# A graph layer on one core: 16 neighbour slots per batch looked up by TensorE in place, features as three 16-bit terms, kept edges on ScalarE

## The chip, the cores and the metric

The kernel runs on 1 core of one Trainium2 chip. The core has five engines with a queue each, which run their instructions in order and wait for each other through semaphores: TensorE (PE in the profile; its weight loads, PEld, overlap its matmuls), VectorE (DVE), ScalarE (ACT), GpSimd (POOL), and SyncE (SP), which issues most transfers. Matmuls write to eight banks of PSUM; everything else lies in SBUF or in the device's memory. The metric is the device time of one execution in microseconds (us). The kernel before takes 1395.76 us, the median of 3 runs (1393.39 to 1398.31).

## The reference

There are 16 graphs of 1024 nodes with 64 features each; the matrix `adj` holds about 8 neighbours per node. Shortened:

```python
h = relu(layernorm(x))                       # per node, 64 features
neigh = (adj > 0) & ~eye
nb = neigh.sum(-1); rank = cumsum(neigh) - neigh
skip = where(nb > 10, (nb + 1) // 2, 1)
rem = neigh & (skip > 1) & (rank % skip == skip - 1) & mask[:, :, None]
rem = rem | rem.T                            # edges dropped, both ways
nd = (neigh | eye) & ~rem                    # what is kept, the node itself included
s = sort(where(nd, h[neighbour], inf))       # per node and feature, over its kept neighbours
agg = 0.25 * quantile(s, .25) + 0.5 * quantile(s, .5) + 0.25 * quantile(s, .75)
y = relu((h + agg) @ W1 + b1) @ W2 + b2
return x + y * mask
```

So for every node the features of its kept neighbours are fetched, sorted for each of 64 features, and combined with weights that depend on the number of neighbours.

## The kernel before

The work goes batch by batch (a batch is one graph, 0 to 15), and two batches make a pair, 0 to 7. A batch is *prepared* and a pair gets its *results*; the results of one pair run beside the preparation of the next but one.

**Preparation** of a batch (`prepare`). `load` brings in `adj`, takes its signs on ScalarE (L1087) and transposes them by a transfer into `ne`. `drop` ranks the edges on TensorE (`rk`, L1174 and L1179), turns them into a distance on ScalarE (`dist`, L1189) and marks the dropped ones on VectorE (`rem`, L1190). `keep` subtracts the marks from the edges on TensorE (`kp`, L1202 to L1206): half of the results are compared on VectorE against the edges themselves (L1209, where the matmul with `plus` is left out), the other half go through ScalarE (L1213, after that matmul), and both give `kept`, which TensorE packs into codes of 17 numbers per 128 columns (`code`, L1216, copied by L1221). `order` sorts the nodes by their number of neighbours and builds the permutation `perm` (L1259). `normalize` computes the features `xt` and packs them beside the codes into `pack`, as one 16-bit half and two bytes, each as a 16-bit number (192 columns, L1425 and L1426). `collect` multiplies `perm` with `pack` (`codeP`, L1286, 332 columns, one tile of 128 nodes after the other), so that codes, node numbers and features arrive in sorted order, and VectorE's maxima (L1295, L1326) turn the codes into lists of neighbours (`idx`). ScalarE copies the node's own features out (L1299, L1303, L1304).

Sorted in this way, a row tile (0 to 7) holds 128 nodes of like degree. `FULL` is the number of neighbour slots of each row tile, 11 down to 4; row tile 0 has its own buffer `g0`, 1 to 3 share `g1`, 4 and 5 `g4`, 6 and 7 `g6`. Each slot of each row tile of each batch is filled by one **gather**, an indirect transfer that GpSimd issues (L1491, 128 rows of 64 numbers from the table `gtab` in memory), or by TensorE: `choose` does so for 8 slots of row tile 0. It spreads the list entries over the partitions (`rowsT`, L1526; `rows`, L1532), compares them with the node numbers into one-hot matrices (`hot`, L1536, in the buffer `wide`, which `rem` and `perm` use too), and multiplies these with the features (`got`, L1548: for each slot 8 matmuls of 192 columns). ScalarE puts half and bytes together in `stage` (L1565, L1566), and two transfers per batch carry that to `g0`. In the last pair `pick` does the same for 40 slots (L1601 to L1632).

**Results** of a pair (`results`, `aggregate`). VectorE sorts the slots with a network of minima and maxima (L1656 to L1664), ScalarE multiplies the slots in the window of quantiles with their coefficients (L1679), TensorE adds them (`acc`, L1685). The sum, as three 16-bit terms `o`, goes back to the original order (`high`: for each row tile one matmul for two terms on 128 columns of the array, L1813, and one for the third on 64, L1814) and through the two layers (`hp`, L1843; `yp`, L1860). The 32 nodes of highest degree have slots of their own (`gg`, L1906).

**What sets the order.** The program is written with generators that are woven together; then `arrange` takes all instructions, derives which waits for which, assigns costs and places them on the five queues by list scheduling. The order of each queue is then fixed. A gather also waits for its predecessor's issue and, by the `leash`, for an instruction of VectorE or ScalarE that the plan puts 25 us earlier. `opened` puts a tiny write (`pause`, L938) behind most of VectorE's operations. `FILL` names places on TensorE's queue, counted by position, where matmuls are put whose results nobody reads (all of line 914). `over` records whether a row tile has a node with more neighbours than slots or fewer than `LEAST`; if so, a second, slower kernel runs after this one (`dense_layer`).

## Time and profile before

| | |
|---|---|
| median of the runs | 1395.76 us (1393.39 to 1398.31) |
| span of the profiled execution | 1391.1 us, 31056 instructions |
| between its span and the runs' median | 4.7 us |
| mean granted TensorE clock | 0.978 |
| gathers on GpSimd (L1491) | 856, 1066 ns each |
| one-hot comparisons on VectorE (L1536, L1611) | 112 and 40, 489 and 487 ns each |

The profiled execution has no time of its own in the records beside its span; the runs that were timed are others. How to read the rows: a group has its line, engine, operation, what it writes and reads, the shape, the count, the busy time in us and the mean in ns, then the idle time of the engine before it and who ended it. A wait has who waited for whom, the total in us, the number of times and the longest. A window has its length, then for each engine the busy us and in brackets the instructions, then the granted clock, the DMA share and GB/s; a window of one line leaves out the engines that don't run it. A matmul's duration includes the drain of the array, so matmuls that follow each other overlap, and the distance of their starts tells more than their length.

### The profile page before, as it was taken

The numbers are of one execution on the slowest core, as the hardware profiler recorded it, in microseconds if no ns is written. First come the engines' busy times: TensorE is split into PE (matmuls) and PEld (weight loads), VectorE is DVE, ScalarE is ACT, GpSimd is POOL, SyncE is SP. The second block draws the span as 40 slices with busy tenths as digits, with TensorE's granted clock in tenths as the row PEclk, the third lists the DMA queues.
The fourth block names the chain that finished last, engine by engine and source line by source line (L and its number), as shares of the span: only waits on it lengthen the run. The fifth ranks groups of instructions, "written<-read, shape, count | busy, mean of one in ns | idle before, by whom it ended". The sixth has DMA issues, their size and how long they took to land. (4 is left out here: it accounts for less than half of the span.)

```text
span 1391.1 us, 31056 instructions
## 1 busy us (share of the span) xinstructions
PE 1266.4 (91%) x9400; PEld 760.6 (55%) x9479; DVE 1171.7 (84%) x4995; ACT 982.6 (71%) x3158; POOL 954.3 (69%) x895
## 2 busy tenths in 40 slices
PE   6868889899999998999998999889998999999996
PEld 4445566566455645565464646546456656544533
DVE  6849987997899789987897986998999779997963
ACT  6787989899579957997398846779479832552062
POOL 0177775677777776777777766777777767776730
PEclk9999999999999999999999999999999999999997
DMA  7998486585995499569947379762952576165101
GB/s 235 243 257 213 114 217 159 151 210 129 205 188 152 93 208 252 112 147 229 224 91 195 97 146 229 161 175 55 230 105 78 110 167 124 29 109 106 37 15 25
DMA packets 376082, 209.42 MB, mean 151 GB/s; under 512 B 328126, under 2 KB 328674, under 8 KB 375906
## 3 DMA queue, kind: packets, MB, share of 16 engines
q1 hardware_dynamic: 347426, 178.15, 53.7%
q0 software_dynamic: 28480, 29.20, 11.0%
q8 instruction: 76, 1.25, 0.4%
q14 instruction: 100, 0.82, 0.2%
HBM read 105.63 MB, written 42.61 MB: 107 GB/s over the span
## 5 line engine op out<-in xcount | busy, mean ns | idle before, releaser
L1491 POOL DMA_INDIRECT g<-gtab,idx x856 | 912.6, 1066 | 368.0 <-DMA g<-gtab,idx 138.6
L1659 DVE TENSOR_TENSOR g<-g 128x256 f32<-128x256 f32 (+5 forms) x479 | 292.0, 620 | 4.9 <-ACT g L1632 2.0
L1664 DVE TENSOR_TENSOR g<-g 128x384 f32<-128x384 f32 (+5 forms) x479 | 290.8, 619 | 5.3 <-PE acc L1739 4.5
L1679 ACT ACTIVATE g<-g,coef 128x64 f32<-128x64 f32 x896 | 244.9, 354 | 34.4 <-DVE g L1659 19.3
L1087 ACT ACTIVATE signs<-at,near 128x1024 fp8e4<-128x1024 f32 x120 | 138.6, 1163 | 51.6 <-DMA at<-in_adj_dram 43.9
L1286 PE MATMUL codeP<-pack,perm 128*128 128x332 bf16 x1024 | 169.4, 310 | 2.2 <-DVE perm L1259 1.1
L1189 ACT ACTIVATE dist<-rk,bias 128x512 f16<-128x512 f32 x256 | 156.7, 726 | 10.0 <-DVE hot L1536 6.2
L1685 PE MATMUL acc<-g,kf 128*128 128x128 f32 (+4 forms) x528 | 133.5, 376 | 17.7 <-ACT g L1679 15.0
L1286 PEld LDWEIGHTS <-perm 128*128 128x128 bf16 x1024 | 92.4, 99 | 83.6 <-issue 24.7
L1179 PEld LDWEIGHTS <-ne 128*128 128x128 fp8e4 x1024 | 79.9, 98 | 67.8 <-issue 29.7
L1209 DVE SCALAR_TENSOR_TENSOR kept<-kp,ne 128x512 fp8e4<-128x512 f32 x132 | 89.8, 686 | 27.5 <-PE kp L1206 19.4
L1174 PE MATMUL rk<-parts,cnt 128*128 128x512 bf16 x239 | 91.7, 384 | 21.0 <-ACT dist L1189 16.2
L1685 PEld LDWEIGHTS acc<-g,kf 128*128 128x128 f32 x528 | 81.9, 195 | 45.4 <-ACT g L1679 35.5
L1814 PE MATMUL high<-at_p,o 128*64 128x512 bf16 x256 | 102.5, 406 | 4.1 <-issue 4.0
L1206 PE MATMUL kp<-kw,rem 128*128 128x128 fp8e5 x1024 | 104.3, 219 | 0.0
L1179 PE MATMUL rk<-kw,ne 128*128 128x128 fp8e5 x992 | 101.4, 221 | 1.1 <-issue 0.2
L1548 PE MATMUL got<-pack,hot 128*128 128x192 bf16 x896 | 92.8, 256 | 7.8 <-DVE hot L1536 5.3
L1203 PE MATMUL kp<-rem,kw 128*128 128x512 bf16 x256 | 97.2, 380 | 1.6 <-DVE rem L1190 1.0
L938 DVE MEMSET pause<- 128x1 bf16 x1630 | 96.2, 59 | 0.0
L1206 PEld LDWEIGHTS <-rem 128*128 128x128 bf16 x1024 | 75.3, 97 | 37.3 <-issue 1.6
L1190 DVE TENSOR_SCALAR rem<-dist,half 128x1024 bf16<-128x1024 f16 x128 | 64.7, 512 | 34.1 <-ACT dist L1189 28.7
L1813 PE MATMUL high<-at_p,o 128*128 128x512 bf16 x237 | 92.0, 390 | 0.9 <-ACT own L1304 0.5
(236 smaller groups left out, 2426.9 us busy)
## 6 DMA issues: line engine op xcount, KB each, us to landing
at<-in_adj_dram SPq DMA_DIRECT2D x122, 512.0 KB
perms<-perm SPq DMA_DIRECT2D x16, 2048.0 KB
g<-gtab,idx POOLq DMA_INDIRECT x856
xt<-in_x_dram SPq DMA_DIRECT2D x16, 256.0 KB
y<-in_x_dram SPq DMA_DIRECT2D x16, 256.0 KB
gtab<-xt SPq DMA_DIRECT2D x16, 256.0 KB
out_dram<-y SPq DMA_DIRECT2D x14, 256.0 KB
spare<-in_adj_dram SPq DMA_DIRECT2D x6, 512.0 KB
```

The costliest lines, as they stand in the source:

```text
L1087: nc.scalar.activation(signs.bitcast(FP8).rearrange("p (n e) -> p e n", e=2), whole.rearrange("p (e n) -> p e n", e=2), AF.Sign, bias=near ...
L1179: run.append(nc.tensor.matmul(rk[:, s * P:(s + 1) * P], ne[:, s, ts, n], twice[:, :P] if not b and n else upper, start=False, stop=(s == 3 ...
L1189: nc.scalar.activation(to, rk, AF.Abs, bias=bias[:, t:t + 1])
L1203: run.append(nc.tensor.matmul(kp, minus, rem[:, 4 * n:4 * n + 4, ts], start=side, stop=False))
L1206: run.append(nc.tensor.matmul(kp[:, s], rem[:, t, at:at + P], minus, start=False, stop=(s == 3)))
L1286: run.append(nc.tensor.matmul(flat, perm[:, t, k * P:(k + 1) * P], pack[:, t], start=False, stop=(t == NT - 1), skip_group_check=True,))
L1491: ins = nc.gpsimd.indirect_dma_start(out=gathered[m, tiles][:, slot, k - lo, h], out_offset=None, in_=tables[2 * m + h][0], in_offset=bass ...
L1659: nc.vector.tensor_tensor(at(f + k * df, df, many), pa, pb, OP.min if what == "<" else OP.max)
L1664: nc.vector.tensor_tensor(pa if back else pb, pa, pb, OP.max if what == "<" else OP.min)
L1679: nc.scalar.activation(v[:, i, j], v[:, i, j], AF.Copy, scale=w[:, i, j:j + 1])
L1685: nc.tensor.matmul(acc, ident32, lines[:, s], start=False, stop=(s == now[-1] and not ends), skip_group_check=True)
L1814: run.append(nc.tensor.matmul(high[C * (k % 2):C * (k % 2) + C], o[:, k, 2 * C:], one, start=False, stop=(k == NT - 1), skip_group_check=True,
```

## The change

- **Slots.** `SERVED` replaces `EARLY` and `EXTRA`: TensorE looks up 8 slots of row tile 1 and 8 of row tile 2 in every batch but the last two, where it was 8 of row tile 0. The function `served` does it in groups of 8 slots, for `choose` and `pick` alike. The looked-up features go straight into `g1` (`to_lines`); `stage` and its transfers are gone. `g1` keeps two buffers, `g0` goes from two to one. Per pair, 94 gathers are issued in place of 110; in all, 744 in place of 856.
- **Terms.** `split` writes the features as three 16-bit terms whose sum is the feature: a cast on ScalarE, a subtraction on VectorE, twice. The matmuls for the three terms add up in the same 64 columns of the bank. For a lookup that is 24 matmuls of 64 columns for a slot where 8 of 192 stood; for `codeP` 8 of 204 columns and 16 of 64 per row tile where 8 of 332 stood. Two row tiles of `codeP` now share a bank, and one copy takes own features and node numbers out of both.
- **Kept edges.** From batch 1 on all of `kept` goes through ScalarE, with the matmul of `plus` each time; on VectorE remain 12 of 132.
- **One-hot rows.** `hot` has two buffers of its own with four of the eight node tiles each; `dist` and `rows` share three buffers in place of two.
- **Beside these:** `LEAST` rises to the smallest counts, and `places` gives the slots whose coefficient can be other than zero: 800 products in place of 896. The sums of `high` go in fours: four matmuls on the whole array, then four on half of it. `aggregate` takes row tiles 0 to 3 first in every pair. `h1` is computed in place. `FILL` is empty.

On TensorE, where the sums go back to the original order, this stood before:

```order
L1813 LDWEIGHTS o
L1813 MATMUL high<-at_p,o 128x512
L1814 LDWEIGHTS o
L1814 MATMUL high<-at_p,o 64x512
L1813 LDWEIGHTS o
L1813 MATMUL high<-at_p,o 128x512
L1814 LDWEIGHTS o
L1814 MATMUL high<-at_p,o 64x512
L1241 LDWEIGHTS kb
L1241 MATMUL ps<-more,kb 128x192
```

and this stands now (the same matmuls, L1744 in place of L1813 and L1749 in place of L1814):

```order
L1744 LDWEIGHTS o
L1744 MATMUL high<-at_p,o 128x512
L1744 LDWEIGHTS o
L1744 MATMUL high<-at_p,o 128x512
L1744 LDWEIGHTS o
L1744 MATMUL high<-at_p,o 128x512
L1749 LDWEIGHTS o
L1749 MATMUL high<-at_p,o 64x512
L1749 LDWEIGHTS o
L1749 MATMUL high<-at_p,o 64x512
L1749 LDWEIGHTS o
```

The half-array matmuls no longer alternate with the full ones; four of a kind stand together.

In `keep`, VectorE had its comparisons between operations of the sort before:

```order
L1209 SCALAR_TENSOR_TENSOR kept<-kp,ne 128x512
L1664 TENSOR_TENSOR g_9867<-g_9867 128x512
L938 MEMSET pause 128x1
L1209 SCALAR_TENSOR_TENSOR kept<-kp,ne 128x512
L1656 TENSOR_TENSOR g_9867<-g_9867 128x256
L938 MEMSET pause 128x1
L1659 TENSOR_TENSOR g_9867<-g_9867 128x2x256
L938 MEMSET pause 128x1
L1209 SCALAR_TENSOR_TENSOR kept<-kp,ne 128x512
L1664 TENSOR_TENSOR g_9867<-g_9867 128x2x256
```

Now they are ScalarE's, between coefficient products (L1604), the packing of codes (L1184) and the casts of `split` (L1374, L1376):

```order
L1604 ACTIVATE g_11224<-g_11224,coef 128x64
L1374 CAST pack<-xt 128x8x64
L1176 ACTIVATE kept<-kp 128x512
L1184 CAST pack<-code 128x136
L1176 ACTIVATE kept<-kp 128x512
L1376 CAST pack<-xt 128x8x64
L1176 ACTIVATE kept<-kp 128x512 x2
L1184 CAST pack<-code 128x136
L1604 ACTIVATE g_11224<-g_11224,coef 128x64
L1176 ACTIVATE kept<-kp 128x512
L1604 ACTIVATE g_11224<-g_11224,coef 128x64
L1176 ACTIVATE kept<-kp 128x512
```

The comparisons moved to another engine, and that engine's queue now holds all 16 of a batch.

On VectorE the two subtractions of `split` stand among operations of the sort:

```order
L1375 TENSOR_TENSOR xt<-xt,pack 128x512
L1588 TENSOR_TENSOR g_9020<-g_9020 128x384
L906 MEMSET pause 128x1
L1583 TENSOR_TENSOR g_6966<-g_6966 128x2x384
L906 MEMSET pause 128x1
L1583 TENSOR_TENSOR g_9020<-g_9020 128x3x128
L906 MEMSET pause 128x1
L1377 TENSOR_TENSOR pack<-xt,pack 128x8x64
L1588 TENSOR_TENSOR g_6966<-g_6966 128x2x384
```

Three operations of the sort stand between the one and the other.

The diff, cut to its core:

```diff
@@ -65,10 +65,9 @@
 CAPS = (13, 11, 11, 10, 9, 8, 7, 6)
 CLASSES = (((0,), 13), ((1, 2, 3), 11), ((4, 5), 9), ((6, 7), 7))
 
-LEAST = (8, 4, 4, 4, 4, 4, 0, 0)
-EARLY, AHEAD = 8, 20
+LEAST = (10, 9, 8, 7, 4, 4, 4, 0)
+SERVED, AHEAD = (0, 8, 8, 0, 0, 0, 0, 0), 20
 FINAL = (8,4,4,4,0,0,0,0)
-EXTRA = {}
 MANY = 10
 TURN = 1
 
@@ -79,38 +78,7 @@
-FILL = {
...
+FILL = {}
...
                 kp = bank([P, 4, P], F32, name="kp", tag="mx" if b or n else "agg", bufs=3 if b or n else 2)
-                side = bool(b in range(16) and n or not b and t % 2)
+                side = bool(not b and (n or t % 2))
                 run = [] if side else [nc.tensor.matmul(kp, plus, ne[:, :, ts, n], start=True, stop=False)]
                 run.append(nc.tensor.matmul(kp, minus, rem[:, 4 * n:4 * n + 4, ts], start=side, stop=False))
                 for s in range(4):
...
-            owns[b // 2] = wk.tile([P, NT, 2, C], F32, name="own", bufs=1)
+            owns[b // 2] = wk.tile([P, NT, 2, C + VALUES - OWN], F32, name="own", bufs=1)
...
-                flat = bank([P, PACKED], F32, name="codeP", tag="code", bufs=3)
...
+                if k == first or not k % 2:
+                    two = min(2 - k % 2, last - k)
+                    flat = bank([P, two, VALUES + C], F32, name="codeP", tag="code", bufs=3)
+                    run = []
+                    for q in range(two):
+                        run.append(nc.tensor.matmul(
+                            flat[:, q, :KEYS], ones16, base[:, :KEYS], start=(q == 0), stop=False, skip_group_check=True
+                        ))
+                        for t in range(NT):
+                            one = perm[:, t, (k + q) * P:(k + q + 1) * P]
+                            last_one = t == NT - 1 and q == two - 1
+                            run.append(nc.tensor.matmul(
+                                flat[:, q], one, pack[:, t, :VALUES + C], start=False, stop=False, skip_group_check=True,
+                            ))
+                            for n in (1, 2):
+                                run.append(nc.tensor.matmul(
+                                    flat[:, q, VALUES:], one, pack[:, t, VALUES + n * C:VALUES + n * C + C], start=False,
+                                    stop=last_one and n == 2, skip_group_check=True,
+                                ))
+                    settle(run)
+                    nc.scalar.copy(own[:, k:k + two, b % 2], flat[:, :, OWN:])
+                    begun = k
...
-                nc.scalar.copy(st[:, k], flat[:, OWN:VALUES])
...
-                nc.scalar.copy(halves[:, :, 1], flat[:, VALUES:VALUES + C])
-                nc.scalar.copy(bytes_[:, :, 0:2], flat[:, VALUES + C:].rearrange("p (c k) -> p c k", k=2))
...
+    def split(h, to):
+
+        nc.scalar.copy(to[:, :, 0:C], h)
+        nc.vector.tensor_tensor(h, h, to[:, :, 0:C], OP.subtract)
+        nc.scalar.copy(to[:, :, C:2 * C], h)
+        nc.vector.tensor_tensor(to[:, :, 2 * C:3 * C], h, to[:, :, C:2 * C], OP.subtract)
...
-        halves, bytes_ = (h.rearrange("p t c -> p (t c)").bitcast(d).rearrange("p (t c k) -> p t c k", t=NT, c=C) for d in (BF16, U8))
-        nc.scalar.copy(pack[:, :, VALUES:VALUES + C], halves[:, :, :, 1])
...
+        split(h, pack[:, :, VALUES:])
+        yield 0.1
...
-                nc.sync.dma_start(out=gathered[m, tiles][:, slots - 1, :, h], in_=owns[m][:, lo:lo + n, h])
-                for k in tiles:
-                    stage, s = staged.pop((2 * m + h, k), None), 0
...
-                        nc.sync.dma_start(
-                            out=gathered[m, tiles][:, order[s]:order[e - 1] + 1, k - lo, h], in_=stage[:, s:e]
...
+                nc.sync.dma_start(out=gathered[m, tiles][:, slots - 1, :, h], in_=owns[m][:, lo:lo + n, h, VALUES - OWN:])
...
     def begun_with(b, k):
 
-        return EARLY if not k else LEAST[k] if any(k in some for some in EXTRA.get(b, ())) else 0
+        return SERVED[k]
+    def served(some, index, given, by, of):
+
+        n = len(some)
+        rows = wk.tile([P, n, P], F16, name="rows", tag="dist", bufs=3)
+        for at in range(0, n, 4):
+            tp = bank([P, 4, P], F32, name="rowsT", tag="mx", bufs=3)
+            settle([
+                nc.tensor.matmul(
+                    tp[:, q], index(at + q).to_broadcast([P, P]), by, start=(q == 0), stop=(q == 3), skip_group_check=True,
+                )
+                for q in range(4)
+            ])
+            nc.scalar.copy(rows[:, at:at + 4], tp)
+        yield 0.5
+        got = bank([P, n, C], F32, name="got", tag="code", bufs=3)
+        for lo in (0, 4):
+            hot = wk.tile([P, 4, n, P], BF16, name="hot", bufs=2)
+            for j in range(4):
+                opened(nc.vector.tensor_scalar(hot[:, j], rows, first[:, lo + j:lo + j + 1], None, OP.is_equal))
+                yield 0.45 * n / 8
+            settle([
+                nc.tensor.matmul(
+                    got[:, q], hot[:, j, q], of(q)[:, lo + j, i * C:i * C + C], start=(q == lo == j == i == 0),
+                    stop=(q == n - 1 and lo + j == NT - 1 and i == 2), skip_group_check=True,
+                )
+                for q in range(n) for j in range(4) for i in range(3)
+            ])
+        given(0, got)
+        yield 1.0
 
     def choose(b):
 
-        for some in ((0,), *EXTRA.get(b, ())):
...
-            hot = wk.tile([P, NT, n, P], BF16, name="hot", tag="wide", bufs=1)
...
-                got = bank([P, 2, 3 * C], F32, name="got", tag="code", bufs=3)
...
+        wanted = [(b % 2, k, s) for k in range(NT) for s in range(SERVED[k])]
+        index = wk.tile([P, len(wanted)], F16, name="index_h", bufs=1)
+        at = 0
+        for k in range(NT):
+            if SERVED[k]:
+                nc.scalar.copy(index[:, at:at + SERVED[k]], lists[b][:, PASSED[k]:PASSED[k] + SERVED[k]])
+                at += SERVED[k]
+        for lo in range(0, len(wanted), 8):
+            some = wanted[lo:lo + 8]
+            yield from served(
+                some, lambda q: index[:, lo + q:lo + q + 1], partial(to_lines, b // 2, some), ident_h,
+                lambda q: pack[:, :, VALUES:],
+            )
+
+    def to_lines(m, some, at, got):
+
+        while at < len(some):
+            h, k, s = some[at]
+            tiles, slots = next(c for c in CLASSES if k in c[0])
+            opening((tiles, slots), m)
+            to = [PLANS[slots][1][some[i][2]] for i in range(at, min(len(some), at + 4)) if some[i][:2] == (h, k)]
+            n = next((n for n in range(2, len(to)) if to[n] - to[n - 1] != to[1] - to[0]), len(to))
+            step = to[1] - to[0] if n > 1 else 1
+            end = to[n - 1] + (1 if step > 0 else -1)
+            line = gathered[m, tiles][:, to[0]:end if end >= 0 else None:step, k - tiles[0], h]
+            nc.scalar.copy(line, got[:, at:at + n])
+            at += n
...
-                            nc.scalar.activation(v[:, i, j], v[:, i, j], AF.Copy, scale=w[:, i, j:j + 1])
+                            if first + k + i in wanted[j]:
+                                nc.scalar.activation(v[:, i, j], v[:, i, j], AF.Copy, scale=w[:, i, j:j + 1])
...
+            run = []
+            for k, s in enumerate(now):
+                some = [j for j in range(size // C) if not by_act or first + k in wanted[j]]
+                if some:
+                    lo, hi = some[0], some[-1] + 1
...
-        for h, half in ((0, 1), (0, 0), (1, 1), (1, 0)) if apart else ((0, 0), (0, 1)) if last else ((0, 1), (0, 0)):
+        for h, half in ((0, 1), (0, 0), (1, 1), (1, 0)) if apart else ((0, 0), (0, 1)):
...
-        for k in some:
-            one = at[k // 2][:, k % 2]
-            run = [nc.tensor.matmul(high, o[:, k, 0:2 * C], one, start=(k == 0), stop=False, skip_group_check=True)]
-            run.append(nc.tensor.matmul(
-                high[C * (k % 2):C * (k % 2) + C], o[:, k, 2 * C:], one, start=False, stop=(k == NT - 1),
-                skip_group_check=True,
-            ))
-            settle(run)
+        for lo in range(some[0], some[-1] + 1, 4):
+            settle([
+                nc.tensor.matmul(
+                    high, o[:, k, 0:2 * C], at[k // 2][:, k % 2], start=(k == 0), stop=False, skip_group_check=True
+                )
+                for k in range(lo, lo + 4)
+            ] + [
+                nc.tensor.matmul(
+                    high[C * (k % 2):C * (k % 2) + C], o[:, k, 2 * C:], at[k // 2][:, k % 2], start=False,
+                    stop=(k == NT - 1), skip_group_check=True,
+                )
+                for k in range(lo, lo + 4)
+            ])
         return high
...
+def places(k):
+
+    most = FULL[k] + 1 + any(host == k for host, _ in HOSTS) + any(guest[0] == k for _, guest, _, _ in GUESTS)
+    return {s for n in range(LEAST[k], most) for at in (n, 2 * n, 3 * n) for s in (at // 4, -(-at // 4))}
```

209 lines of the change are left out of this document (34 added, 175 removed), and 6 rows, old and new, of the table FILL.

## The prediction

> **What bounds the kernel now.** I read the page first, then the stages of 200 us, then who waits on VectorE and on GpSimd, then the timeline of TensorE. The page:
>
> ```profile
> PE 1266.4 (91%) x9400; PEld 760.6 (55%) x9479; DVE 1171.7 (84%) x4995; ACT 982.6 (71%) x3158; POOL 954.3 (69%) x895
> PE 17%; DVE 7%; issue 6%; ACT 4%; DMA 1%; POOL 0%; SPq 0%; DVEq 0%; POOLq 0%; ACTq 0%
> PE high L1814 3%; PE high L1813 2%; DVE g L1659 2%; DVE g L1664 2%; ACT g L1679 2%; PE acc L1685 1%; PE codeP L1286 1%; PE yp L1860 1%; PE hp L1843 1%; DMA g<-gtab,idx 1%; PE rowsT L914 1%; ACT dist L1189 1%; PE high L914 1%; PE rowsT L1601 1%; PE kp L1203 1%
> ```
>
> The chain can be followed back to 886 us only (its shares add up to about 36% of the span). TensorE's 91% is inflated: line 914 is filler that nobody reads. By stages, first all engines, then line 914 alone:
>
> ```profile
> 300.00:500.00 200.00, 186.43 (x1512) 113.29 (x1525) 172.82 (x678) 162.48 (x519) 156.41 (x144) 1.00 0.72 163
> 900.00:1100.00 200.00, 185.66 (x1321) 111.38 (x1331) 181.30 (x726) 156.35 (x538) 153.69 (x140) 0.97 0.58 132
> sum 1200.00, PE 1118.56 PEld 675.89 DVE 1052.42 ACT 872.71 POOL 892.84; mean PE 186.43 PEld 112.65 DVE 175.40 ACT 145.45 POOL 148.81
> sum 1200.00, PE 192.84 PEld 74.47; mean PE 32.14 PEld 12.41
> ```
>
> From 100 to 1300 us the columns are PE, PEld, DVE, ACT, POOL. VectorE is busy 1052 of 1200 us (88%), TensorE without filler about 926 (77%). VectorE is the first bound. GpSimd is the rival:
>
> ```profile
> L1491 POOL DMA_INDIRECT g<-gtab,idx x856 | 912.6, 1066 | 368.0 <-DMA g<-gtab,idx 138.6
>   POOL g L1491: 147.9, 451
>   ACT g L1756: 2.6, 1
> ```
>
> Its 856 gathers with the idle before them fill 1281 us, so it hardly pauses; but the last two rows, those who waited for line 1491, are GpSimd itself and one copy of ScalarE. Gathers land before they are needed. What VectorE does wait for is TensorE and ScalarE (whole run):
>
> ```profile
> DVE keys L1295 <- PE codeP L1286: 38.0, 26, 5.4
> DVE rem L1190 <- ACT dist L1189: 28.7, 37, 2.9
> DVE kept L1209 <- PE kp L1206: 19.4, 27, 3.0
> DVE hot L1536 <- ACT rows L1532: 8.9, 5, 3.8
> DVE rem L1190 <- PE got L1548: 4.6, 5, 1.9
> DVE kept L1209 <- PE code L1216: 1.8, 3, 0.7
> ```
>
> **The change, part by part.** Prices on VectorE and ScalarE:
>
> ```profile
> L1209 DVE SCALAR_TENSOR_TENSOR kept<-kp,ne 128x512 fp8e4<-128x512 f32 x132 | 89.8, 686 | 27.5 <-PE kp L1206 19.4
> L1213 ACT ACTIVATE kept<-kp 128x512 fp8e4<-128x512 f32 x124 | 78.4, 640 | 5.2 <-PE kp L1206 3.6 <-ACT g L1679 0.4
> L1536 DVE TENSOR_SCALAR hot<-rows,first 128x1024 bf16<-128x1024 f16 x112 | 48.6, 489 | 9.1 <-ACT rows L1532 8.9
> L1664 DVE TENSOR_TENSOR g<-g 128x512 f32<-128x512 f32 x102 | 69.0, 681 | 0.0
> L1304 ACT CAST own<-codeP 128x128 uint8<-128x128 f32 x128 | 37.5, 294 | 0.0
> L1303 ACT CAST own<-codeP 128x64 bf16<-128x64 f32 x128 | 31.6, 247 | 5.6 <-DMA g<-own 5.6
> L1679 ACT ACTIVATE g<-g,coef 128x64 f32<-128x64 f32 x896 | 244.9, 354 | 34.4 <-DVE g L1659 19.3 <-DVE pause L938 9.2 <-DVE g L1664 4.6
> ```
>
> *Kept edges.* 120 of the 132 comparisons on VectorE go to ScalarE: 120 x 0.686 = 82.3 us off VectorE, 120 x 0.640 = 76.8 onto ScalarE, and each takes one more 512-column matmul. The waits in front of the comparisons go with them: the two rows above and smaller ones, 24 us in all x 120/132 = 22. I take -22; bounds -24 and 0 (if the sort that follows is late instead). But the phase gets longer for its batch: ScalarE then has 16 x 0.640 plus 8 casts, some 12.5 us, where now TensorE sets it with about 10 (24 matmuls of 512 columns, 64 of 128 and 64 of 17, at the spacings below).
>
> *One-hot rows.* 152 become 264: 112 x 0.489 = +54.8 us on VectorE. *Three terms.* Two subtractions of 512 columns for each of 18 feature tiles: 36 x 0.681 = +24.5. So VectorE's work stays: -82.3 + 54.8 + 24.5 = -3 us. The rows for the one-hots come from ScalarE in twice as many groups, so that wait of 8.9 doubles: +9. Each subtraction waits for a cast, but three sort operations stand between them: +3, bounds 0 and 36 x 0.6 = 22.
>
> *ScalarE* gains 76.8; it loses the pair of own copies (128 x 0.541 = 69) against 65 longer ones, 96 coefficient products (96 x 0.354 = 34) and half the copies out of the lookup banks. It ends some 20 to 40 us lower and is not the bound at 71%. But TensorE waits 14.8 us for those own copies (row below): -10, bounds -15 and 0.
>
> *One-hot buffers of their own.* The next batch's rem no longer waits for the lookup to leave the shared wide buffer: the 4.6 us above go, and in the first 300 us, where batches follow each other at the length of that buffer's turn, I take as much again and a little: -13 in all, bounds -20 and 0.
>
> *TensorE.* Timeline rows (start, us, last field the count):
>
> ```profile
>   PE codeP L1282: 14.8, 14
> 213.63 0.38 PE L1202 MATMUL kp<-ne,kw 128*128 128x512 fp8e4 x1
> 213.85 0.38 PE L1203 MATMUL kp<-rem,kw 128*128 128x512 bf16 x1
> 214.07 0.39 PE L1206 MATMUL kp<-kw,rem 128*128 128x128 fp8e5 x4
> 214.29 0.34 PE L1149 MATMUL nb<-kb,cnt 128*128 128x1 bf16 x8
> 700.93 3.96 PE L1548 MATMUL got<-pack,hot 128*128 128x192 bf16 x46
> 984.00 0.38 PE L1813 MATMUL high<-at_p,o 128*128 128x512 bf16 x1
> 984.31 0.40 PE L1814 MATMUL high<-at_p,o 128*64 128x512 bf16 x1
> 984.64 0.39 PE L1813 MATMUL high<-at_p,o 128*128 128x512 bf16 x1
> 211.39 1.19 PE L1138 MATMUL cp<-ne,kw 128*32 128x512 fp8e4 x16
> L1286 PEld LDWEIGHTS <-perm 128*128 128x128 bf16 x1024 | 92.4, 99 | 83.6 <-issue 24.7
> ```
>
> A row's length is the spacing plus the drain of the last. Matmuls of 512 columns start 0.22 us apart (213.63, 213.85; 0.215 without the rounding). 46 lookups in 3.96 us are 0.083 apart; four of 128 columns, 0.39 with a drain near 0.22, are 0.056 apart; eight of one column, each with a full 128x128 load of 16-bit weights, (0.34 - 0.17)/7 = 0.025. A 64-column matmul lies between: 0.025 to 0.056, and I take 0.029 (half the 0.056 and a trifle). So 6336 of them are 184 us against 1216 x 0.083 = 101: +83. The packed matmul becomes 204 + 64 + 64 columns: some 0.147 against 0.141, +6. Kept: 120 x 0.215 = +26. Rows: +6. Against it, the sums: full and half matmuls alternate 0.31 and 0.33 us apart, 0.64 to 0.65 a pair where two of 512 columns back to back would take 0.43. In fours a switch comes a quarter as often: (8 x 0.215 + 0.22)/4 = 0.485 a pair, 256 x 0.165 = -42; if two halves on different columns run together, as the 16 of L1138 do (four quarters of 512 columns pass in 0.27), -70. On the chain the two lines hold 3% + 2.4%, 75 us, of which a quarter goes: -20, bounds 0 and -32. The longer lookups: of +83 two thirds are hidden by the stages in which TensorE has 23% to spare, and the kept matmuls likewise: +20, bounds 0 and 115.
>
> Each of the 7168 added pairs has its own weight load, recorded at 0.099 us (last row above). The eight of L1149 follow each other at 0.025, so loads hide behind each other. The Trainium skill (TensorE: Matmul & The Clock Gate, LDWEIGHTS) charges a load P / 1.2 ns, 0.107 us for 128 columns, which speaks against three matmuls on the same weights; in line, that would put TensorE's +83 at about +640.
>
> *Filler.* It goes altogether. On the chain it holds about 2% (28 us), half of it where TensorE would wait anyway: -14. What it covered is the clock:
>
> ```profile
> 541.70:545.10 3.40, 1.26 (x9) 0.59 (x9) 3.40 (x19) 0.38 (x2) 0.48 (x2) 1.00 0.88 244
> 545.10:548.50 3.40, 2.59 (x17) 2.29 (x18) 3.40 (x13) 3.40 (x10) 2.79 (x3) 0.50 1.04 208
> 869.30:872.70 3.40, 1.86 (x22) 1.01 (x25) 3.29 (x12) 3.39 (x6) 2.79 (x3) 1.00 1.15 221
> 1060.50:1063.90 3.40, 1.00 (x14) 0.58 (x12) 3.40 (x14) 3.21 (x19) 2.49 (x4) 1.00 0.12 28
> 1063.90:1067.30 3.40, 2.71 (x14) 2.27 (x15) 3.40 (x18) 3.27 (x17) 2.79 (x3) 0.50 0.15 28
> ```
>
> A stretch of 3.4 us with TensorE busy for 1.0 or 1.26 us is followed by one at half clock (0.50); one with 1.86 is not. Such a half-clock stretch takes 1.7 us of matmul time. The 193 us of filler, about 1.5 us in a stretch that it saves, can be holding up to 125 stretches; since the lookups fill some, I take 30, and half of them on the path: 30 x 1.7 / 2 = +25, bounds 0 and 125 x 1.7 / 2 = 106. The same page of the Trainium skill (The HAM clock gate) has this window, 3413 ns, but halves the clock only after an idle one; here a third of a window's work was not enough to keep it. By the page's reading the term would be near 0 and the forecast 25 us lower; the measured rows decide.
>
> *GpSimd.* 112 gathers fewer, 119 us by the row above, and 28 fewer transfers on SP. Nobody waits for them, so -4; bound -119.
>
> **Sum:** -22 - 3 + 9 + 3 - 10 - 13 - 20 + 20 - 14 + 25 - 4 = -29 us, and the sort's order, no longer set by the 110 gathers of a pair but by VectorE, should leave it idle less: at 90% in place of 88% over the 1200 us, -12 that no row bounds from the other side than 0 and 1200 x 7% = -84 (VectorE at 95%). Together -41: a span of 1350. The median of the runs lies 4.7 us above the profiled span of 1391.1, so 1355.
>
> **Rivals.** (A) *GpSimd was the pace.* For: it never rests. Against: the rows of those who waited. Then most of the 119 us is gained until VectorE's own 1169 us with its idle start and end binds, about -85: 1310. (B) *The clock, or the supply of matmuls.* Without filler the clock drops in more stretches than I took: from 80 on the path, 80 x 1.7 = 136 in place of 25, the sum turns over: 1391 - 66 + 136, or some 1465; break-even at 39 on the path. The same sign has the lookup if 96 matmuls with their loads can't be kept 0.029 apart in so long a run (none longer than 46 is in the trace): at 0.056 it is +254 in place of +83, and a fourth of the difference on the path gives 1398. If every load took its 0.099 in turn, 7168 x 0.07 = 502 us more would make TensorE the bound over the 1200 us (926 + 83 + 502 - 42 = 1469), some 1660; the rows leave that 0.02 of B. Together I put this side at 1425. (C) *A new wait takes the place.* The kept phase, longer by 2.5 us in 15 batches, is on the path of preparation: +37, and the gain is gone: 1393. That the fallback runs instead is excluded: the smallest counts in the reference's inputs, by row tile, reach the new floors.
>
> **Chances.** My forecast 0.49, A 0.14, B 0.24, C 0.13 (which is no change for 0.08, slower for 0.03, faster for 0.02). Three runs spread over 0.35%, so 0.3% (4 us) is what can be told from no change. Faster 0.65, same 0.08, slower 0.27. The likeliest's own range is 1320 to 1385; both signs are open, so the range reaches from A to B: 1300 to 1425.
>
> **What would show it.** VectorE's busy time within 10 us of 1172 and no kept line among its waits but batch 0's; the wait on codeP down; sums in groups of about 1.7 us for four pairs; 64-column lookups 0.03 us apart over 96; a mean clock of 0.93 to 0.97; GpSimd at about 835 us with pauses. I am wrong if the mean clock is under 0.92, if VectorE waits for lookups or rows for over 30 us, or if its share from 100 to 1300 us stays under 88%.

## The result and the profile after

The changed kernel takes 1379.99 us (median of 12 runs, 1364.04 to 1394.56) where the kernel before takes 1396.96 (12 runs, 1390.32 to 1400.78). The ratio is 0.9845, with a 95% interval from 0.9814 to 0.9877: 21.6 us or 1.55% faster. The medians differ by 17.0 us only, because the ratio leaves out four of the changed kernel's runs (1384.83 to 1394.56) that lie over 1.5% above its fastest. The profiled execution has a span of 1372.9 us against 1391.1, so 18.2 us less. The forecast was 1355 us.

The page of the changed kernel, in the same order as before (busy time by engine, then the chain by engine and by line):

```profile
PE 1156.4 (84%) x16135; PEld 854.2 (62%) x16135; DVE 1162.3 (85%) x5133; ACT 980.6 (71%) x2883; POOL 848.7 (62%) x783
PE 37%; ACT 22%; issue 13%; DVE 12%; DMA 12%; SPq 3%; POOL 1%; DVEq 0%; ACTq 0%; POOLq 0%
PE got L1493 10%; DMA at<-in_adj_dram 9%; ACT dist L1152 5%; ACT kept L1176 4%; ACT g L1604 4%; PE acc L1615 3%; DVE g L1583 3%; PE high L1744 3%; ACT signs L1050 3%; DVE g L1588 2%; PE codeP L1254 2%; PE rk L1137 2%; PE rk L1142 2%; PE row
```

VectorE's work fell by 9.4 us (1171.7 to 1162.3), so 8.8 of the 18.2 us are idle time that it lost. The lookups (`got`, L1493) are now the first line of the chain, and the loads of `adj` (`at`) the second, with 9% of the span. (The chain of before reaches back to 886 us only, so the two can't be compared line by line.) From 100 to 1300 us VectorE is as busy as before, 1052 of 1200 us (87.7%):

```profile
sum 1200.00, PE 1034.62 PEld 767.40 DVE 1051.97 ACT 884.41 POOL 802.30; mean PE 172.44 PEld 127.90 DVE 175.33 ACT 147.40 POOL 133.72
```

What VectorE waits for after the change (total in us, times, longest):

```profile
DVE rem L1153 <- ACT dist L1152: 35.8, 37, 3.3
DVE hot L1490 <- ACT rows L1484: 22.0, 10, 4.9
DVE y L1800 <- PE yp L1796: 18.8, 11, 11.9
DVE keys L1269 <- ACT own L1263: 17.9, 13, 3.1
DVE at_e L1215 <- PE ps L1212: 15.9, 12, 2.8
DVE num L1190 <- ACT pack L1184: 13.9, 3, 8.1
DVE hot L1490 <- PE got L1493: 10.4, 8, 1.9
...
DVE pack L1377 <- ACT pack L1376: 2.4, 3, 1.0
```

Against the rows of before, the waits for the kept edges (19.4 and 1.8) are gone, and that for `codeP` fell from 38.0 to 17.9, now ending at the copy of the own features. In their place stand longer waits for the one-hot rows (8.9 to 22.0), for the lookups themselves (new, 10.4), for `dist` (28.7 to 35.8), and, in the sort of the nodes that follows the kept phase, for `ps` and `pack`, which were small before:

```profile
DVE num L1227 <- ACT pack L1221: 8.1, 6, 2.3
DVE at_e L1252 <- PE ps L1249: 6.3, 7, 1.2
```

ScalarE waits longer too, for the loads of `adj`, and SyncE, whose queue issues them, waits at the load of the features until `split` has read the buffer `xt` for the last time (before: until ScalarE had packed it). Before, then changed:

```profile
ACT signs L1087 <- DMA at<-in_adj_dram: 43.9, 34, 3.5
SPq L1406 <- ACT pack L1426: 47.5, 8, 9.3
```

```profile
ACT signs L1050 <- DMA at<-in_adj_dram: 82.8, 41, 8.1
SPq L1381 <- DVE pack L1377: 150.0, 12, 23.4
```

No experiment took these waits apart; whether the longer wait in SyncE's queue is what makes the loads late is not shown.

Where along the run the time went shows when the `perm` matrices are built (VectorE; the last two numbers before the semicolon are the first and the last start), kernel before, then changed:

```profile
L1259 DVE TENSOR_SCALAR perm<-turned,place_f x136: 252/477/689, 44.6 to 1119.1; 128x1024 bf16<-128x1024 f16 x120, 128x128 bf16<-128x128 f16 x8, 128x896 bf16<-128x896 f16 x8
```

```profile
L1222 DVE TENSOR_SCALAR perm<-turned,place_f x136: 248/481/729, 49.6 to 1152.3; 128x1024 bf16<-128x1024 f16 x120, 128x128 bf16<-128x128 f16 x8, 128x896 bf16<-128x896 f16 x8
```

The last `perm` comes 33 us *later*, and what follows it is 51 us *shorter*. The two stretches by engine (PE, PEld, DVE, ACT, POOL), before:

```profile
0.00:1119.00 1119.00, 1016.18 (x8158) 626.02 (x8221) 955.00 (x4128) 879.92 (x2793) 793.56 (x746) 0.98 0.72 169
1119.00:1391.00 272.00, 250.26 (x1244) 134.58 (x1259) 216.69 (x868) 102.70 (x365) 160.73 (x149) 0.97 0.36 74
```

and changed:

```profile
0.00:1152.00 1152.00, 992.35 (x14341) 741.43 (x14341) 981.73 (x4345) 898.79 (x2613) 723.00 (x671) 0.93 0.69 159
1152.00:1373.00 221.00, 164.00 (x1795) 112.77 (x1795) 180.61 (x789) 81.83 (x271) 125.65 (x113) 0.85 0.46 87
```

Up to the last `perm` VectorE does 27 us more work and idles 170 us in place of 164; behind it, it does 36 us less and idles 40 in place of 55. So more of the sorting is done while batches are still being prepared, and VectorE's net gain is 9 us of work and 15 us of idle time at the end, less 6 us of idle time in the preparation.

### The profile page after: what moved, and what is told of

Same layout as the page of the kernel before. It is cut to its first block, busy times and chain, and to the rows that moved or that the text cites. A ratio compares the mean times of both kernels' runs of the same rounds, so it can differ in the third digit from the quotient of the medians.

```text
span 1372.9 us, 43927 instructions
## 1 busy us (share of the span) xinstructions
PE 1156.4 (84%) x16135; PEld 854.2 (62%) x16135; DVE 1162.3 (85%) x5133; ACT 980.6 (71%) x2883; POOL 848.7 (62%) x783
## 4 chain that ended last, share of the span: by engine, by line
PE 37%; ACT 22%; issue 13%; DVE 12%; DMA 12%; SPq 3%; POOL 1%; DVEq 0%; ACTq 0%; POOLq 0%
PE got L1493 10%; DMA at<-in_adj_dram 9%; ACT dist L1152 5%; ACT kept L1176 4%; ACT g L1604 4%; PE acc L1615 3%; DVE g L1583 3%; PE high L1744 3%; ACT signs L1050 3%; DVE g L1588 2%; PE codeP L1254 2%; PE rk L1137 2%; PE rk L1142 2%; PE rowsT L1479 2%; PE high L1749 2%
## 5 line engine op out<-in xcount | busy, mean ns | idle before, releaser
L1453 POOL DMA_INDIRECT g<-gtab,idx x744 | 809.5, 1088 | 452.3 <-DMA g<-gtab,idx 135.4
L1583 DVE TENSOR_TENSOR g<-g 128x768 f32<-128x768 f32 (+5 forms) x479 | 289.4, 618 | 12.7 <-DMA g<-gtab,idx 6.3
L1604 ACT ACTIVATE g<-g,coef 128x64 f32<-128x64 f32 x800 | 221.9, 379 | 40.5 <-DVE g L1583 18.6
L1493 PEld LDWEIGHTS <-hot 128*128 128x128 bf16 x6336 | 216.9, 99 | 32.5 <-issue 23.4
L1493 PE MATMUL got<-pack,hot 128*128 128x64 bf16 x5376 | 208.8, 194 | 11.2 <-issue 6.8
L1050 ACT ACTIVATE signs<-at,near 128x1024 fp8e4<-128x1024 f32 x120 | 137.9, 1157 | 85.3 <-DMA at<-in_adj_dram 82.8
L1254 PE MATMUL codeP<-pack,perm 128*128 128x204 bf16 x1024 | 173.0, 260 | 6.0 <-DVE perm L1222 6.0
L1258 PE MATMUL codeP<-pack,perm 128*128 128x64 bf16 x2048 | 169.0, 197 | 0.0
L1258 PEld LDWEIGHTS <-perm 128*128 128x128 bf16 x2048 | 162.8, 101 | 4.7 <-issue 2.4
L1176 ACT ACTIVATE kept<-kp 128x512 fp8e4<-128x512 f32 x244 | 155.0, 679 | 2.2 <-PE kp L1169 1.2
L1490 DVE TENSOR_SCALAR hot<-rows,first 128x1024 bf16<-128x1024 f16 x264 | 116.7, 499 | 36.4 <-ACT rows L1484 22.0
L1142 PEld LDWEIGHTS <-ne 128*128 128x128 fp8e4 x1024 | 82.8, 103 | 44.3 <-issue 17.5
L1254 PEld LDWEIGHTS <-perm 128*128 128x128 bf16 x1024 | 100.3, 100 | 15.0 <-DVE perm L1222 10.3
```

Source lines behind the costliest of these rows:

```text
L1050: nc.scalar.activation(signs.bitcast(FP8).rearrange("p (n e) -> p e n", e=2), whole.rearrange("p (e n) -> p e n", e=2), AF.Sign, bias=near ...
L1142: run.append(nc.tensor.matmul(rk[:, s * P:(s + 1) * P], ne[:, s, ts, n], twice[:, :P] if not b and n else upper, start=False, stop=(s == 3 ...
L1176: nc.scalar.activation(kept[:, 4 * n:4 * n + 4], kp, AF.Relu, saturate=False)
L1254: run.append(nc.tensor.matmul(flat[:, q], one, pack[:, t, :VALUES + C], start=False, stop=False, skip_group_check=True,))
L1258: run.append(nc.tensor.matmul(flat[:, q, VALUES:], one, pack[:, t, VALUES + n * C:VALUES + n * C + C], start=False, stop=last_one and n == ...
L1453: ins = nc.gpsimd.indirect_dma_start(out=gathered[m, tiles][:, slot, k - lo, h], out_offset=None, in_=tables[2 * m + h][0], in_offset=bass ...
```

## The experiments

The question was why 18 us of the 41 came. My theory: the terms for the edges and the sums hold, and the loss lies with the longer lookups and the lower clock. Rivals: the clock alone; GpSimd's gathers; the luck of the order that the planner draws. The later loads of `adj` are a rival that no experiment tests.

One fact has to be told first. The experiments ran on four chips. On one the kernel before took 1394.7 us, as in the comparison above; this is called the usual kind. On the three others it took 1693 to 1730 us. What is different there is shown in the second experiment. Numbers near 1 are ratios to the kernel before on the same chip, with their 95% interval, and those of the two kinds of chip are not mixed.

**One term per lookup** (the usual kind of chip). The lookup matmuls of two of three terms are left out, so the features that lookups bring are rounded to 16 bits; the planner's cost for the lookups is kept. Even so the planner drew another order: ScalarE's operations stand in a different order from about 105 us on.

```diff
+        self.busy *= 3 if self.engine == "PE" and self.writes[0].tile.name.startswith("got") else 1
...
-                for q in range(n) for j in range(4) for i in range(3)
+                for q in range(n) for j in range(4) for i in range(1)
```

> The changed kernel with lookups of the first of the three terms alone: 8 matmuls of 64 columns for a slot in place of 24. It leaves out two thirds of the lookup matmuls (4224 with their weight loads; the features it brings are rounded to 16 bits), and with them about 123 us of TensorE's work; everything else is done. Where the kernel before takes 1397 us: my term said that of 83 us more lookup work 20 lie on the path, so a gain of some 30 us over the changed kernel (ratio 0.96); if the lookups lie beside VectorE's work, within 5 us (0.98 to 0.99). Where the kernel before takes about 1700 us: if what is slow there is the feeding of TensorE with instructions, 8448 of 43500 rows fewer give back most of what the lookups lost, ratio 1.03 to 1.08 in place of 1.15; if something else is slow there, 1.13 to 1.15 remains.

Measured: 1349.51 us, ratio 0.9678 (0.9637 to 0.9719). Against the changed kernel's 0.9845 that is 1.67% less, 23 us, with an uncertainty of 7. Its page, its `perm`, its two stretches, and what VectorE waits for at the one-hot matrices:

```profile
PE 1074.5 (80%) x11876; PEld 756.1 (56%) x11911; DVE 1157.9 (86%) x5133; ACT 981.9 (73%) x2883; POOL 860.2 (64%) x783
```

```profile
L1223 DVE TENSOR_SCALAR perm<-turned,place_f x136: 249/482/598, 48.6 to 1128.5; 128x1024 bf16<-128x1024 f16 x120, 128x128 bf16<-128x128 f16 x8, 128x896 bf16<-128x896 f16 x8
```

```profile
0.00:1128.00 1128.00, 921.01 (x10711) 656.08 (x10737) 970.14 (x4319) 893.51 (x2586) 727.47 (x667) 0.89 0.71 162
1128.00:1339.00 211.00, 153.49 (x1168) 99.97 (x1175) 187.78 (x815) 88.38 (x297) 132.75 (x116) 0.82 0.48 91
```

```profile
DVE hot L1491 <- ACT rows L1485: 22.6, 9, 5.2
```

The wait for the lookups (10.4 us) is gone from its list, and 24 of the 33 us by which the last `perm` had moved back are won again; the wait for the rows is as it was. VectorE's work hardly changed (1157.9 against 1162.3), its idle time fell from 211 to 182 us. ScalarE's wait for the loads of `adj` fell by 10 us, from 82.8 to 72.7. The mean clock *fell* from 0.916 to 0.875, and the kernel got faster: a low mean clock doesn't by itself make this kernel slow, though what the stretches at half clock cost is not separated here. GpSimd issues the same 744 gathers, so their number did not hold these 23 us. How much of the 23 us is the other order, and not the lookups, is not shown; the one redrawn order below, on another chip, moved the time by 0.2%, uncertain by 0.7%.

**The filler back in the changed kernel**: 361 matmuls that nobody reads, ahead of 18 banks before which TensorE's trace shows a gap of over 1 us; the order of all else is the same. Three runs, all on chips of the other kind.

```diff
-FILL = {}
+FILL = {
+    ('code', 0): 20,
+    ('code', 6): 30,
+    ('ps', 0): 24,
...
+}
...
+            filler[ins.ins.name] = True
```

> The changed kernel with filler put back: 361 matmuls that nobody reads, ahead of 18 banks of TensorE before which its trace shows a gap of over 1 us, each lot sized to three quarters of its gap; all other instructions keep their order. If the lower clock of the changed kernel (0.916, 60 half-clock stretches of 3.4 us) is what ate the missing gain, a clock of 0.94 to 0.96 brings 10 to 20 us: ratio to before 0.970 to 0.977 in place of 0.985. If the gaps are waits for data and the half-clock stretches behind them lie off the path, the clock rises and the time stays within 4 us: 0.982 to 0.988.

> The same kernel as in the run with filler before (the changed kernel with 361 filler matmuls back, ahead of 18 gaps of TensorE). There the kernel before took 1693 us in place of 1397, with TensorE for stretches of 20 us given a new instruction only every 0.7 us while GpSimd issued gathers, so that nothing could be read on the clock. If that slowness stays, 1.15 of before again. If the kernel before takes 1397 us again: a gain of 10 to 20 us over the changed kernel (0.970 to 0.977) if the lost clock lies on the path, within 4 us of it (0.982 to 0.988) if it lies beside waits for data.

> The changed kernel with 361 filler matmuls back ahead of 18 gaps of TensorE, nothing else moved. My term for the clock was +25 us for 30 half-clock stretches more; the changed kernel has some 48 more than the kernel before. If they are on the path, a clock of 0.94 to 0.96 brings 10 to 20 us: ratio 0.970 to 0.977. If the gaps are waits for data and what follows them at half clock is waited for by nobody, it stays within 4 us: 0.982 to 0.988. The run with one term, faster at a clock of 0.875, speaks for the second.

Measured: 1.1547 (1.1506 to 1.1588) where the kernel before takes 1693 us, 1.1482 (1.1399 to 1.1564) at 1724 us, 1.1426 (1.1387 to 1.1465) at 1730 us. So on these chips a kernel that differs from the changed one by filler alone is 14 to 15% *slower* than the kernel before. On the clock they say nothing (beside the redrawn order below: 1.1547 against 1.1570, which is no difference). What is slow there shows TensorE from 78 to 92 us, in the lookups of the first batch (start, us, count, idle before):

```profile
76.96 1.36 PE L1510 MATMUL got<-pack,hot 128*128 128x64 bf16 x40
78.74 0.28 PE L1510 MATMUL got<-pack,hot 128*128 128x64 bf16 x4 [0.42 <-issue]
79.59 0.19 PE L1510 MATMUL got<-pack,hot 128*128 128x64 bf16 x1 [0.57 <-issue]
...
82.00 0.19 PE L1510 MATMUL got<-pack,hot 128*128 128x64 bf16 x1 [0.54 <-issue]
82.71 0.19 PE L1510 MATMUL got<-pack,hot 128*128 128x64 bf16 x1 [0.52 <-issue]
84.18 0.23 PE L1510 MATMUL got<-pack,hot 128*128 128x64 bf16 x1 [1.27 <-issue]
85.56 0.21 PE L1510 MATMUL got<-pack,hot 128*128 128x64 bf16 x1 [1.15 <-issue]
```

GpSimd meanwhile:

```profile
82.19 0.95 POOL L1470 DMA_INDIRECT g<-gtab,idx  x1 [0.31 <-issue]
83.44 0.95 POOL L1470 DMA_INDIRECT g<-gtab,idx  x1 [0.30 <-issue]
84.69 0.94 POOL L1470 DMA_INDIRECT g<-gtab,idx  x1 [0.30 <-DMA g<-gtab,idx]
```

After 40 matmuls at about 0.03 us, TensorE gets one every 0.7 or 1.4 us, while GpSimd keeps its 1.25 us per gather. The profile shows nothing that TensorE waits for ("issue"), and these matmuls carry no wait of their own. Two stretches of this run, one with gathers and one without, then the same lookups of the changed kernel on the usual chip:

```profile
80.00:100.00 20.00, 3.04 (x16) 1.30 (x17) 0.00 (x0) 0.00 (x0) 15.12 (x17) 0.59 0.44 71
294.00:304.00 10.00, 10.00 (x298) 9.76 (x296) 8.10 (x45) 7.01 (x24) 0.00 (x0) 0.94 0.41 118
```

```profile
78.00:98.00 20.00, 18.07 (x400) 15.37 (x396) 7.83 (x41) 11.09 (x20) 15.43 (x16) 0.91 1.04 208
```

```profile
82.01 3.00 PE L1493 MATMUL got<-pack,hot 128*128 128x64 bf16 x92 [0.30 <-issue]
```

16 matmuls in 20 us beside 17 gathers, 298 in 10 us beside none; on the usual chip 400 in 20 us beside 16 gathers, 92 of them in one row, 0.031 us apart. Over the whole run (starts of the lookup matmuls, those more than 3 us apart left out) they follow each other at some 140 ns on average while a gather is issued and at some 60 while none is; on the usual chip at about 50 in both cases. What it costs are the waits for TensorE (the releasers are less sure here, since this trace has only about half as many semaphore updates as one of the usual chip):

```profile
ACT g L1546 <- PE got L1510: 225.0, 20, 35.8
PE got L1510 <- issue: 208.8, 260, 3.3
DVE hot L1507 <- PE got L1510: 188.3, 26, 29.7
```

**Another order from the planner**: its margin between engines is 60 ns in place of 50. This is the yardstick for all experiments that redraw the order.

```diff
-ROUNDS, LEASH, LATE = 6, 25000, 50
+ROUNDS, LEASH, LATE = 6, 25000, 60
```

> The changed kernel with one number of the planner changed: the margin that it adds between engines is 60 ns in place of 50. The same work; only the order of the instructions on the queues is drawn anew. If the order that the planner finds is luck worth as much as the parts of the change, the time moves by over 0.5% either way (ratio to before under 0.980 or over 0.990). If orders drawn from the same work are alike, it stays at 0.982 to 0.988. The size of this step is the yardstick for every experiment that makes the planner draw a new order.

Measured: 1.1570 (1.1518 to 1.1623), on the chip of the first run with filler (1.1547). The numbers of the expectation were for the other kind of chip; beside the run with filler, which keeps the changed kernel's order, 0.2% is no difference. One redrawn order, on one of these chips, is not worth 1%; it is a single draw, and none was seen on the usual chip.

**The kernel before without its filler**, all else in the same order.

> The kernel before with the filler matmuls alone taken out; every other instruction stands in the same order on its engine. My terms for this part of the change were -14 us (filler off the chain) and +25 us (clock): 11 us slower than before, ratio 1.008, granted clock from 0.978 down to 0.92 or so, as in the changed kernel (0.916). Rival 1, the clock costs far more than I took: 50 us or more slower, ratio from 1.035. Rival 2, the half-clock stretches lie beside other waits: ratio 0.990 to 1.000 although the clock falls.

> The kernel before without its filler, once more. Where the kernel before takes 1397 us: my terms give +11 us (1.008), rival 1 (the clock is worth far more) 1.035 or more, rival 2 (the clock lies beside other waits) 0.990 to 1.000, to which the slow run points (0.995 although the clock fell from 0.916 to 0.85).

Measured: 0.9950 (0.9919 to 0.9981) and 0.9942 (0.9901 to 0.9983), with the clock down from 0.91 or 0.92 to 0.85. My two terms (-14 and +25) made it 11 us slower; it is 8 and 10 us faster (uncertain by 5 and 7). One of the twelve executions of the second run took 3162.6 us and is not in the ratio; nothing on record says why. This was seen only where TensorE starves for instructions, so for the usual chip it is a hint.

**The sums back in turns**, one matmul on the whole array and one on half of it, all else in the same order.

```diff
-            settle([
+            turned_runs.append([
...
+                for k in range(lo, lo + 4) for whole in (True, False)
```

> The changed kernel with the matmuls of the sums back in turns (one on the whole array, one on half of it, and so on) in place of four and four; the same instructions, and every engine's other instructions in the same order. My term was -20 us for the fours, bounds 0 and -32: so 20 us slower than the changed kernel, ratio to before 0.999. Rival, the sums lie beside VectorE's work in the results and cost nothing on the path: ratio 0.985. Either way a pair of matmuls should take 0.64 us again where the changed kernel has about 0.44.

Measured: 1.1712 (1.1659 to 1.1766). Beside the run with filler that is 28 us more (uncertain by 11), beside the redrawn order 24 (by 13). TensorE's groups, kernel before and changed kernel on the usual chip:

```profile
L1814 PE MATMUL high<-at_p,o 128*64 128x512 bf16 x256 | 102.5, 406 | 4.1 <-issue 4.0
L1813 PE MATMUL high<-at_p,o 128*128 128x512 bf16 x237 | 92.0, 390 | 0.9 <-ACT own L1304 0.5 <-issue 0.2
```

```profile
L1744 PE MATMUL high<-at_p,o 128*128 128x512 bf16 x256 | 78.7, 412 | 0.9 <-ACT o L1903 0.9
L1749 PE MATMUL high<-at_p,o 128*64 128x512 bf16 x256 | 43.6, 420 | 0.0
```

By the starts of the matmuls at full clock, the next one starts 0.216 us after one on the whole array, 0.31 when a half follows a whole, 0.31 to 0.34 when a whole follows a half, and 0.004 when a half follows a half on other columns. A pair so takes 0.65 us in turns (also in this experiment) and about 0.38 in fours. So TensorE is spared some 70 us (256 x 0.27), and 24 to 28 of them were on the path of that chip.

**Kept edges shared again** between VectorE and ScalarE.

```diff
-                side = bool(not b and (n or t % 2))
+                side = bool(b in range(16) and n or not b and t % 2)
```

> The changed kernel with the kept edges shared between VectorE and ScalarE again, as in the kernel before; the planner draws a new order. My terms: VectorE has 82 us more work and its waits of 22 us ahead of the comparisons again, ScalarE 77 us less: some 60 to 100 us slower if VectorE's queue is the end of all, ratio 1.03 to 1.05. Rival, the preparation is what is late (perm of batch 15 came 33 us later than before), and the kept phase with all on ScalarE is the longer way through it: then the split is faster, 0.965 to 0.98.

Measured: 1.1559 (1.1479 to 1.1639), beside 1.1482 (1.1399 to 1.1564) for the run with filler on that chip: 0.8% slower, uncertain by 1.2%. VectorE's work rose by 65 us (to 1229.4), but at 61% it bounds nothing there. The planner drew a new order for this run. It is inconclusive for the usual chip.

**Half of the lookups**: 8 slots of row tile 1 alone, 112 gathers more. Three runs, all on chips of the other kind.

```diff
-SERVED, AHEAD = (0, 8, 8, 0, 0, 0, 0, 0), 20
+SERVED, AHEAD = (0, 8, 0, 0, 0, 0, 0, 0), 20
```

> The changed kernel with TensorE serving 8 slots of row tile 1 alone; 112 gathers more on GpSimd (856 again), 112 one-hot comparisons and 112 x 24 matmuls fewer. If the lookups and the waits they brought on VectorE (rows and got, 32 us, and 55 us of comparisons) cost more than the gathers that they spare: 20 to 60 us faster, ratio 0.94 to 0.97. If the shorter end of the run comes from GpSimd having 112 gathers less (theory A of the prediction): 20 to 50 us slower, ratio 1.00 to 1.02.

> The changed kernel with TensorE serving 8 slots of row tile 1 alone, once more. Where the kernel before takes 1397 us: 20 to 60 us faster than the changed kernel (ratio to before 0.94 to 0.97) if the 112 comparisons, 2688 matmuls and the waits they bring on VectorE cost more than the 112 gathers they spare; 20 to 50 us slower (1.00 to 1.02) if the shorter end of the run comes from the gathers spared. Where the kernel before takes about 1700 us again, TensorE's count of instructions decides: half of the lookups gave back a third of the 15% there, so 1.10 again.

> The changed kernel with TensorE serving 8 slots of row tile 1 alone: 112 gathers more (856 again), 112 one-hot comparisons (55 us of VectorE) and 2688 lookup matmuls fewer. In the run with one term, 4224 lookup matmuls fewer gave 23 us over the changed kernel; by that, 2688 fewer give 15, and VectorE's 55 us less work some 25 to 55 more: ratio 0.93 to 0.96, faster than either kernel. If the gathers spared are what shortens the changed kernel (theory A), the 119 us more of them turn it over: 1.00 to 1.02.

Measured: 1.1035 (1.0945 to 1.1124), 1.1081 (1.1031 to 1.1131) and 1.1044 (1.0996 to 1.1092). Beside the runs with filler on the same chips (1.1482, 1.1426) that is 77 us less (uncertain by 21) and 66 (by 11): 112 gathers more cost less than 2688 lookup matmuls with their one-hot comparisons, where the matmuls starve. VectorE's work falls to 1126.5 us in the first of them, by 36, where the expectation had 55. Whether it beats the changed kernel on the usual chip wasn't seen; nor was the changed kernel itself run on the other chips, where its nearest relatives stand for it.

## Why the prediction came out right, step by step

Direction and range held; of the 41 us of the sum 18 came (profiled spans), 22 by the ratio, 17 by the medians. That the total fits is in part luck. Several terms were off, and they offset each other; and all three signs of being wrong came: the mean clock was 0.916 (named: under 0.92), the waits for lookups and rows 32.4 us (over 30), and VectorE's share from 100 to 1300 us 87.7% (under 88).

- *Kept waits (-22)*: right, the rows are gone; all waits ahead of these comparisons were 27.5 us by the group's row, where the prediction counted 24. But rival C, the longer kept phase, came in part beside it: the waits for `pack` and `ps` behind that phase grew by 5.8 and 9.6 us. The term stood, and those waits were priced at nothing.
- *VectorE's work (-3)*: -9.4. *Rows (+9)*: +13.1. *Split (+3)*: 2.4 for the row shown; the 150 us that SyncE's queue waits at the same subtraction were not in the sum. *TensorE's wait for own copies (-10)*: the 14.8 us are gone, but TensorE now waits 10.5 us at the same place for VectorE's maxima; VectorE's own wait for `codeP` fell by 20.
- *Sums (-20)*: the right size. Halves on different columns do run together, so TensorE is spared some 70 us, my upper figure; 24 to 28 us lay on the path of the one chip where it was undone. On the usual chip the term was not measured.
- *Lookups (+20 of +83)*: the size fits. Leaving out 123 us of them (4224 matmuls at 0.029 us) gave 23, so 83 are worth some 16, if the other order of that run is worth nothing. What I had not named is how: VectorE waits for the two `hot` buffers (10.4 us), and the whole preparation moves back.
- *Filler (-14) and clock (+25)*: by the mean clocks TensorE ran some 230 us at half clock, where it was some 60 before: about 50 stretches of 3.4 us more, not the 30 of the sum. Even so 0.875 went with a faster kernel, and taking the filler out of the kernel before gave 8 to 10 us on the other chips, where the two terms together had cost 11. There the two were some 20 us too dear; which of them, and what they are on the usual chip, stays open.
- *The steps that failed* are "wide buffer freed" (-13) and "VectorE less idle" (-12), together 25 us for idle time that VectorE was to lose beside the waits priced one by one. (The second was also summed wrongly: 90% in place of 88% of 1200 us are 24 us, not 12.) The waits that were to go went: those for the kept edges, some 20 us of that for `codeP`, and the 4.6 us on the lookup. But others took their place: `ps` and `pack` (+15.4), the lookups (+10.4), `dist` (+7.1), and rows by 4 us more than the sum had. So VectorE lost 8.8 us of idle time in all, and from 100 to 1300 us none. For `dist` I read it so: the next batch's `rem` is free earlier and then waits for ScalarE, which itself waits for TensorE's ranks (23.0 us in the second row below; before, 10.0 us of idle time in all, most of it for the one-hot matrices). I took the order of the sorts to be set by the gathers. The run with one term speaks for the lookups as what holds VectorE, since its idle time falls by 29 us when they are a third as long, with all 744 gathers there; the other order of that run and the later loads of `adj` stay as rivals.

```profile
L1189 ACT ACTIVATE dist<-rk,bias 128x512 f16<-128x512 f32 x256 | 156.7, 726 | 10.0 <-DVE hot L1536 6.2 <-PE rk L1179 2.0 <-DVE pause L938 0.9
```

```profile
L1152 ACT ACTIVATE dist<-rk,bias 128x512 f16<-128x512 f32 x256 | 156.5, 710 | 28.9 <-PE rk L1142 23.0
```

- *Waits for lookups and rows*: 32.4 us are +24 against before, of which the sum had 9.
- *Rival A (GpSimd was the pace)*: it fell. 112 gathers fewer went with 22 us, not 85, and the run with one term brought as much again without touching them.
- *Rival B (the supply of matmuls)*: on the usual chip it fell, since lookups start 28 to 29 ns apart through runs of 92 (median over the run), and the weight loads hide. On three of four chips of the experiments it is what happens, not by the weight loads but by how seldom TensorE gets an instruction; and at 14 to 16% over the kernel before, for the nearest relatives of the changed kernel, it is far more than the 2% (1425 us) that I gave this side. My forecast holds for the kind of chip on which the trace of before was taken; nothing in that trace told the other.

## What to carry to other kernels

Price work that is moved to an engine "with room" by who waits for its last result: 83 us of lookups on an engine that is busy three quarters of the time still cost about a fifth of that here (worked out from the run with one term). Count instructions as well as busy time: three matmuls of 64 columns (3 x 0.029 us) take about as long as one of 192 (0.083) and are three times as many to be fed, and where a chip fed them slowly, the changed kernel's nearest relatives were some 15% slower where the changed kernel itself was 1.5% faster on the usual chip. A mean clock is no verdict (0.875 went with a faster kernel than 0.916): ask whether the matmuls at half clock are waited for. And look at every engine's waits, the transfer queue's too, before you price an operation by the engine that runs it.

## What the runs showed of the hardware

- On three chips TensorE, waiting for nothing that the profile shows, got a matmul only every 0.7 or 1.4 us in stretches of up to 20 us while GpSimd issued gathers every 1.25 us (from 80 to 100 us 16, 11 and 16 matmuls in the three runs with filler, with 17 gathers in each). The block transfers of instructions don't tell the kinds apart (instructions' queue: packets, MB, share), filler run there, then the changed kernel on the usual chip:

```profile
q8 instruction: 131, 2.15, 0.5%
```

```profile
q8 instruction: 128, 2.10, 0.7%
```

  The Trainium skill (Runtime: NRT & Kernel Launch, Instruction fetch mechanics) has blocks of 16 KiB fetched ahead and the cost mostly hidden; the size agrees (2.15 MB in 131 packets), and in the run with filler no block of that queue arrives between 80.2 and 110.0 us, so the starving from 80 to 100 us lies within a stretch without such a transfer. What causes it stays open. The traces of these chips hold only 15 to 16 thousand semaphore updates, whatever the kernel, where the usual chip has 27 to 31 thousand; so the recording itself may be what is short of room there. That is a guess, and no run tests it.
- A window's work does not have to be near nothing for the clock to be halved (changed kernel; us, PE busy, ..., granted clock):

```profile
318.50:321.90 3.40, 1.53 (x6) 0.68 (x4) 3.40 (x23) 1.53 (x6) 2.48 (x4) 1.00 1.23 258
321.90:325.30 3.40, 2.52 (x21) 2.20 (x22) 1.77 (x10) 3.40 (x10) 2.62 (x3) 0.50 1.13 247
386.80:390.20 3.40, 1.77 (x7) 0.55 (x8) 1.62 (x7) 1.87 (x4) 0.58 (x1) 1.00 1.38 219
390.20:393.60 3.40, 1.69 (x14) 1.05 (x15) 3.40 (x15) 1.63 (x2) 0.00 (x0) 1.00 1.10 183
393.60:397.00 3.40, 3.40 (x14) 1.09 (x11) 2.26 (x10) 0.61 (x4) 0.00 (x0) 0.50 0.83 178
```

  1.77 us of 3.40 kept the full clock, 1.69 and 1.53 did not: in these stretches about half of the window is needed. Counted over this whole trace in steps of 3.41 us from one change of the clock: all 26 steps at full clock with under 1.6 us of TensorE's work were followed by half clock, 5 of 26 with 1.7 to 2.5 us, and none of 276 with more.
